# An attention and mixture-of-experts layer: experts' results with slots on partitions, added up in the output's rows by transfers

## The chip, the cores and the metric

The kernel runs on one core of a Trainium2 chip. The metric is the device time of one execution in microseconds. The core has TensorE (PE, matmuls and transposes through it, results in PSUM), VectorE (DVE), ScalarE (ACT), GpSimd (POOL) and SyncE (SP); transfers (DMAs) are issued by SP, ACT and POOL and carried by 16 DMA engines. Each engine works through its own queue in order, and waits on semaphores for the others.

## The reference

The input x has 16 sequences of 256 tokens with 128 channels, 4096 tokens in all. The result is x plus an attention branch and a mixture-of-experts branch, both on the normalised x. Cut to what matters:

```python
xn = layernorm(x)                                  # per token
# attention: 16 heads of 8 channels, causal, relu on q, k, v
att = softmax(mask(q @ k.T / sqrt(8))) @ v + xn
att = gamma * normalise(att) + beta
# experts: RMS norm, 8 experts, the best two per token
h = rms_weight * xn * rsqrt(mean(xn**2) + 1e-6)
w, i = top_2(softmax(h @ gate_w.T)); w = w / w.sum()
for each expert e:
    eo[e] = (silu(h @ w1[e].T) * (h @ w3[e].T)) @ w2[e].T
out = x + att + xn + sum over the token's two experts of w * eo[e]
```

An expert has 448 hidden units. A token's expert output thus counts for the two experts that it was routed to, 8192 results of 128 channels in all.

## The kernel before, in words

**Layout.** Tokens lie on partitions, 32 token tiles of 128, in 8 blocks of four (`BT`). The first part of the kernel normalises x (`normed`, `exact`), routes tokens (`route`), and writes each token's normalised row, its number and its weight into the list of each of its two experts (`scattered`): the dram tensor `lists` has rows of 130 floats, 128 channels, the token's place (`C`) and its weight (`C + 1`), and is filled by indirect transfers from POOL (L612). The place is made by an iota (L604): row p * 32 + t for partition p of token tile t. Places that no token fills hold numbers from 4096 on (`filling`).

**Attention.** The main loop runs over 16 units `u`, two halves of the heads for each of the 8 blocks. A unit has scores and their maxima, `weights` (three parts: ScalarE's exponentials `e`, from unit 3 on with the causal mask by POOL's L884), `values` (L899, L910) that read the masked `e`, and `finish` (L929 transposes, VectorE normalises). TensorE's order is the program's own, written by hand; a scheduler orders the other engines. Between pieces of a unit, `fill` puts other work: normalisation, logits, steps of the experts and one step of `rest`.

**Experts.** `experts` is a generator with three steps for each of 36 tiles of 256 list places (more, if the routing needs them, in a branch at the end). `fetch` loads a tile's rows (`frows`) and the expert's weights by SP, two tiles ahead. `turned_rows` transposes the rows (L1112). `up` multiplies by w1 and w3 (L1123), and ScalarE and VectorE form `hid` (L1131, L1132, L1134), hidden units on partitions. `down` multiplies by w2 (L1140): w2 is the stationary operand, the result has channels on partitions and the 256 places in columns, and ScalarE copies it to SBUF as `yT` (L1148). `deliver`, one step later, transposes `yT` back by two PE transposes (L1154), so that places lie on partitions, VectorE multiplies by each place's weight (`fres`, L1156), and POOL issues two indirect transfers with accumulation (L1160), 128 rows of 512 B each, into rows of the dram tensor `places`. As a token has results in two tiles, a tile's transfers wait until those of the tile before have landed; within a tile they don't wait for each other.

**PSUM.** `misc` has two buffers in turn, for logits, projections, transposes, `values`, and here the down product and the transposed result. `fres` and `yT` have two buffers each.

**Rest of the layer.** `rest(n0, n1)` normalises the attention result of blocks n0 to n1 (small VectorE operations, then ScalarE L1218, L1223 and VectorE L1219, L1224, L1225) and leaves in `y` everything of the output but the experts' part. It runs a step at a time beside the main loop from block 5 on: `rest(0, 4)` from then, `rest(4, 6)` in the last unit, `rest(6, 8)` after it, a step for each remaining step of the experts.

**Beginning and end.** `places` is zeroed by nine SP stores (L269, L272), the ninth for the 256 rows that unfilled places write to. At the end, behind the last scatter, eight transfers by SP and ACT load `places` in the order of `y` (L1370), VectorE adds (L1374), and SP and ACT store to `out` (L1375).

Of the kernel before, what the change touches and what calls it, by code (L numbers as in the profile page):

```python
# [9 lines left out]
F32 = mybir.dt.float32  # L10
# [4 lines left out]
ALU = mybir.AluOpType  # L15
AX = mybir.AxisListType

P = 128
# [8 lines left out]
def tile_attention_plus_moe(  # L27
# [31 lines left out]
    nc = tc.nc  # L59
    V, S, G, T = nc.vector, nc.scalar, nc.gpsimd, nc.tensor  # L60

    NTOK, C = x.shape
    NT = NTOK // P
# [3 lines left out]
    NCI = w2T.shape[2]  # L67
    I = CI * NCI
    BT = 4
    BW = BT * P  # L70
    NB = NT // BT
# [17 lines left out]
    SL = 256  # L89
# [16 lines left out]
    y = const.tile([P, NT, C], F32, name="y")  # L106
# [71 lines left out]
    ident = const.tile([P, P], F32, name="ident")  # L178
# [78 lines left out]
    nought = const.tile([P, BW], F32, name="nought")  # L257
# [6 lines left out]
    G.memset(taken, 0.0)  # L264
    lists = tc.dram_tile([E * CAP + SL, RW], F32, name="lists")

    places = tc.dram_tile([NTOK + SL, C], F32, name="places")
    for a in range(0, NTOK, BW):
        nc.sync.dma_start(  # L269
            out=places[a : a + BW, :].rearrange("(p t) c -> p (t c)", p=P), in_=nought  # L270
        )
    nc.sync.dma_start(  # L272
        out=places[NTOK : NTOK + SL, :].rearrange("(p t) c -> p (t c)", p=P),
        in_=nought[:, 0 : SL // P * C],
    )
    fill_ins = nc.sync.dma_start(
        out=lists[E * CAP : E * CAP + SL, :].rearrange("(a p) w -> p a w", p=P), in_=filling
    )
# [27 lines left out]
    def misc(name):  # L306
        return psM.tile([P, BW], F32, tag="misc", name=name)
# [275 lines left out]
    def scattered(part, t0, at_u, wts):  # L583

        t1 = ROUTES[part][1]
        for b0 in range(t0, t1, 2 * BT):
            blocks = range(b0, min(b0 + 2 * BT, t1), BT)  # L590
            rows = {}
            for r in range(2):
                for b in blocks:
                    if r == 0:
                        rows[b] = norm.tile([P, BT, RW], F32, tag="rows", bufs=4, name=f"rows_{b}")
                        for t in range(BT):
                            S.activation(
                                rows[b][:, t, 0:C],
                                xn[:, b + t, :],
                                AF.Copy,  # L600
                                scale=rstd[:, b + t : b + t + 1],
                            )
                    if r == 0:
                        G.iota(  # L604
                            rows[b][:, :, C].bitcast(I32),
                            [[1, BT]],
                            base=b,
                            channel_multiplier=NT,
                        )
                    G.tensor_copy(rows[b][:, :, C + 1], wts[:, r, b - t0 : b - t0 + BT])  # L610
                    for t in range(BT):
                        ins = G.indirect_dma_start(  # L612
                            out=lists,
                            out_offset=bass.IndirectOffsetOnAxis(
                                ap=at_u[:, r, b - t0 + t : b - t0 + t + 1], axis=0
                            ),
                            in_=rows[b][:, t, :],
                            in_offset=None,
                        ).ins
                        tc.declare_no_dep(  # L620
                            ins, group="lists", reason="lists' rows are written once"
                        )
                        tc.add_to_no_dep_group("lists", ins)
                        tc.add_to_no_dep_group(f"rows of part {part}", ins)
                        yield ins
# [188 lines left out]
    turned = {}  # L814
# [246 lines left out]
    def experts(ffn, i0, i1):  # L1061
# [3 lines left out]
        NH = SL // P  # L1065
# [69 lines left out]
            return h  # L1135

        def down(i, hid, w2, rows):
            yp = misc(f"Y_{i}")[:, :SL]
            for c in range(NCI):
                T.matmul(  # L1140
                    yp,
                    lhsT=w2[:, 0, c, :],
                    rhs=hid[c // 2][:, ts(c % 2, SL)],
                    start=(c == 0),
                    stop=(c == NCI - 1),
                )
            yT = ffn.tile([P, SL], F32, tag="yT", bufs=2, name=f"yT_{i}")
            S.copy(yT, yp)  # L1148
            return yT, rows

        def deliver(i, yT, rows):
            tp = misc(f"R_ps_{i}")[:, :SL].rearrange("p (a c) -> p a c", c=C)
            for a in range(NH):
                T.transpose(tp[:, a, :], yT[:, ts(a, P)], ident)  # L1154
            res = ffn.tile([P, NH, C], F32, tag="fres", bufs=2, name=f"fres_{i}")
            V.tensor_tensor(  # L1156
                res, tp, rows[:, :, C + 1 : C + 2].to_broadcast([P, NH, C]), ALU.mult
            )
            for a in range(NH):
                ins = G.indirect_dma_start(  # L1160
                    out=places,
                    out_offset=bass.IndirectOffsetOnAxis(
                        ap=rows[:, a, C : C + 1].bitcast(U32), axis=0
                    ),
                    in_=res[:, a, :],
                    in_offset=None,
                    compute_op=ALU.add,
                ).ins
                tc.declare_no_dep(
                    ins, group=f"results of tile {i}", reason="a list has a token once"  # L1170
                )
                tc.add_to_no_dep_group(f"results of tile {i}", ins)
            behind["POOL"] = ins
# [1 line left out]
        got = {i: fetch(i) for i in range(i0, min(i0 + 2, i1))}  # L1175
        yield
        hT = turned_rows(i0, got[i0][0])
        late = turned = None
        for i in range(i0, i1):
            if turned is not None:  # L1180
                deliver(*turned)
            rows, w1, w3, w2 = got.pop(i)
            if i + 2 < i1:
                got[i + 2] = fetch(i + 2)
            hid = [up(i, 0, hT, w1, w3)]
            yield
            if late is not None:
                turned = (late[0], *down(*late))
            if i + 1 < i1:
                next_hT = turned_rows(i + 1, got[i + 1][0])  # L1190
            yield
            hid.append(up(i, 1, hT, w1, w3))
            hT = next_hT
            late = (i, hid, w2, rows)
            yield
        if turned is not None:
            deliver(*turned)
        turned = (late[0], *down(*late))
        yield
        deliver(*turned)  # L1200

    rstd2 = const.tile([P, NT], F32, name="rstd2")
    nmean2 = const.tile([P, NT], F32, name="nmean2")
# [1 line left out]
    def rest(n0, n1):  # L1205

        t0, t1 = n0 * BT, n1 * BT
        lv = small.tile([P, t1 - t0], F32, tag="lv", name=f"lv_{n0}")
        V.tensor_scalar(lv, mv[:, t0:t1, 1], LN2_EPS, None, ALU.add)
        _, rl = yield from newton_sqrt(lv[:], t1 - t0, "l")  # L1210
        nm = small.tile([P, t1 - t0], F32, tag="nm", name=f"nm_{n0}")
        V.scalar_tensor_tensor(nm, mv[:, t0:t1, 0], -1.0, rl, ALU.mult, ALU.mult)
        yield
        for n in range(n0, n1):
            yn = y[:, ts(n, BT), :]
            for t in range(n * BT, n * BT + BT):
                i = slice(t - t0, t - t0 + 1)
                S.activation(y[:, t, :], y[:, t, :], AF.Identity, bias=nm[:, i], scale=rl[:, i])  # L1218
            V.tensor_tensor(yn, yn, gamma_sb.unsqueeze(1).to_broadcast([P, BT, C]), ALU.mult)  # L1219
            yield  # L1220
            for t in range(n * BT, n * BT + BT):
                by, mean = agains[t]
                S.activation(xn[:, t, :], xn[:, t, :], AF.Identity, bias=mean, scale=by)  # L1223
            V.tensor_tensor(yn, yn, beta_sb.unsqueeze(1).to_broadcast([P, BT, C]), ALU.add)  # L1224
            V.tensor_tensor(yn, yn, xn[:, ts(n, BT), :], ALU.add)  # L1225
            yield


    def chain(*parts):
# [70 lines left out]
    for u in range(len(units)):  # L1300
        n, r = units[u]
# [41 lines left out]
            side["rest"] = rest(0, 4) if n == 5 else rest(4, 6)  # L1343
    side["rest"] = chain(side["rest"], rest(6, 8))
    for _ in side["experts"]:
        next(side["rest"], None)
    for _ in side["rest"]:
        pass

# [10 lines left out]

    early.__exit__(None, None, None)
    late_pool.__exit__(None, None, None)
    last = ctx.enter_context(tc.tile_pool(name="last", bufs=NB, reuse_waits="tile"))
    ov = out.rearrange("(t p) c -> p t c", p=P)
    pv = places[0:NTOK, :].rearrange("(p t) c -> p t c", p=P)
    zs = []
    for n in range(NB):
        z = last.tile([P, BT, C], F32, tag="z", name=f"z_{n}")
        eng = nc.sync if n % 2 == 0 else nc.scalar
        eng.dma_start(out=z, in_=pv[:, ts(n, BT)])  # L1370
        zs.append(z)
    for n in range(NB):
        yn = y[:, ts(n, BT), :]
        V.tensor_tensor(yn, yn, zs[n], ALU.add)  # L1374
        (nc.sync if n % 2 == 0 else nc.scalar).dma_start(out=ov[:, ts(n, BT), :], in_=yn)  # L1375


# [50 lines left out]
```

## Time and profile before

| what | value |
| --- | --- |
| median of 6 runs | 646.78 us (644.81 to 651.02) |
| the profiled execution's own time | 648.49 us |
| its span | 646.7 us |
| granted TensorE clock, mean | 0.935 of full |
| busy: PE, DVE, ACT, POOL | 542.8, 432.9, 338.3, 265.5 us |
| POOL's accumulating scatters, L1160 | 72 of 1.589 us in the mean, 3.3 us from issue to landing (median) |
| zeroing stores, L269 | 8 of 256 KB, 3.1 us to landing |
| first and last of L1160 issued | 181.7 and 627.3 us |

How to read the lines: times are microseconds from the span's start. A group's line has the source line, engine, operation, tiles (output <- input), shapes and count; then busy time in all and mean nanoseconds of one; then the time that the engine stood idle just before, and what ended most of it. An f32 matmul is recorded as two instructions, a transpose as one. In a timeline's line the brackets hold the idle time before it and what ended it; that releaser is inferred, and of several it is the one seen last. A row by stage has, after its borders and length, the busy time and count of PE, of PE's weight loads, DVE, ACT and POOL, then the granted clock, the share of the DMA engines and GB/s. An "issue" of a POOL transfer is the time in which POOL makes its descriptors; the transfer lands later.

### The profile page before, as it was taken

The page shows a single profiled execution, that of the slowest core. Times are in us where ns is not written, and L with a number is a line of the kernel's source. Part 1 is how long each engine was busy: PE and PEld are TensorE (multiplying, and loading weights), DVE is VectorE, ACT ScalarE, POOL GpSimd, SP SyncE. Part 2 cuts the span into 40 slices and gives each one's busy share as a digit, 9 for nine tenths or more (in the row PEclk, how much of TensorE's full clock was granted, in tenths as well). Part 3 has the DMA queues.
Part 4 walks back from the last instruction along what each step waited for, and adds up shares of the span by engine and source line. Part 5 has one row for each costly group of instructions (what it writes and reads, how often), then busy time and mean ns, then how long its engine had stood idle before and what let it go on. Part 6 is the DMA issues. An engine that isn't in the chain of part 4 may idle for free. (4 is left out here: it accounts for less than half of the span.)

```text
span 646.7 us, 9948 instructions
## 1 busy us (share of the span) xinstructions
PE 542.8 (84%) x3269; PEld 322.7 (50%) x3283; DVE 432.9 (67%) x1153; ACT 338.3 (52%) x677; POOL 265.5 (41%) x311
## 2 busy tenths in 40 slices
PE   3587879669988889899999999899989998999920
PEld 1244434335655545565556555555655565666610
DVE  6758688655577866868576847693787556665833
ACT  1534796456527446564555455536478554446520
POOL 4240027730125866566435332444235342445440
PEclk9796779779989989999999999999999999999975
DMA  6200001143023433353333324232332232435128
GB/s 196 106 1 1 2 16 42 51 137 102 15 45 88 116 84 73 87 127 89 87 85 67 71 60 103 60 67 64 95 73 60 60 67 69 103 63 119 14 25 260
DMA packets 45893, 49.34 MB, mean 76 GB/s; under 512 B 5840, under 2 KB 38224, under 8 KB 45840
## 3 DMA queue, kind: packets, MB, share of 16 engines
q1 hardware_dynamic: 30112, 37.40, 19.4%
q0 software_dynamic: 12416, 8.99, 10.0%
q10 hardware_dynamic: 3312, 2.30, 1.2%
q8 instruction: 27, 0.44, 0.3%
q14 instruction: 26, 0.21, 0.1%
HBM read 34.16 MB, written 14.50 MB: 75 GB/s over the span
## 5 line engine op out<-in xcount | busy, mean ns | idle before, releaser
L1160 POOL DMA_INDIRECT places<-fres,frows x72 | 114.4, 1589 | 115.3 <-DVE fres L1156 82.4
L1123 PE MATMUL AG<-hT,w 128*112 128x256 f32 x576 | 143.5, 394 | 8.2 <-PE R_ps L1154 5.4
L884 POOL TENSOR_SCALAR_AFFINE_SELECT e<-e 128x512 f32<-128x512 f32 (+1 forms) x78 | 70.2, 950 | 153.4 <-ACT e L881 152.8
L1123 PEld LDWEIGHTS AG<-hT,w 128*112 128x112 f32 x576 | 100.3, 182 | 43.6 <-issue 10.9
L881 ACT ACTIVATE e<-W 128x1024 f32<-128x1024 f32 x96 | 93.4, 1020 | 38.9 <-PE W L855 25.8
L1132 DVE SCALAR_TENSOR_TENSOR th<-th,AG 112x512 f32<-112x512 f32 x72 | 49.4, 686 | 74.5 <-ACT th L1131 73.6
L805 DVE TENSOR_REDUCE tops<-S 128x4 f32<-128x1024 f32 x64 | 75.3, 1217 | 32.8 <-PE S L783 32.8
L1131 ACT ACTIVATE th<-AG 112x512 f32<-112x512 f32 x72 | 42.7, 593 | 66.2 <-PE AG L1123 65.7
L1140 PE MATMUL Y<-hid,w 112*128 112x256 f32 x288 | 70.2, 386 | 6.4 <-DVE Qs L823 3.1
L612 POOL DMA_INDIRECT lists<-rows,ratu_c x64 | 64.8, 1012 | 21.9 <-issue 14.7
L770 PE MATMUL S<-KTm,QT 32*128 32x256 f32 (+1 forms) x512 | 70.6, 545 | 3.5 <-DVE tops L805 2.3
L855 PE MATMUL W<-Qm,KT 32*128 32x512 f32 (+1 forms) x512 | 61.7, 536 | 3.0 <-DVE tops L805 2.3
L1140 PEld LDWEIGHTS Y<-hid,w 112*128 112x128 f32 x288 | 52.1, 190 | 21.7 <-PE q_ps L700 4.3
L1134 DVE TENSOR_TENSOR hid<-th,AG 112x512 f32<-112x512 f32 x72 | 48.9, 679 | 1.6
L770 PEld LDWEIGHTS S<-KTm,QT 32*128 32x128 f32 x512 | 31.4, 194 | 24.1 <-issue 12.1
L920 ACT COPY oT<-O 128x512 f32<-128x512 f32 x32 | 18.7, 584 | 46.3 <-PE O L910 46.3
L899 PE MATMUL O<-e,vstat 128*32 128x512 f32 x256 | 36.1, 634 | 8.1 <-DVE rs L940 4.7
L797 DVE TENSOR_REDUCE tops<-S 128x8 f32<-128x1024 f32 x32 | 37.6, 1216 | 2.1 <-PE S L783 2.1
L783 PE MATMUL S<-cmask,ident_bf 128*128 128x256 bf16 (+1 forms) x192 | 37.4, 319 | 0.0
L1148 ACT COPY yT<-Y 128x256 f32<-128x256 f32 x36 | 13.3, 369 | 40.9 <-PE Y L1140 40.7
L855 PEld LDWEIGHTS W<-Qm,KT 32*128 32x128 f32 x512 | 24.7, 190 | 18.0 <-issue 5.5
L783 PEld LDWEIGHTS <-ident_bf 128*128 128x128 bf16 x192 | 15.1, 99 | 35.9 <-issue 31.5
(241 smaller groups left out, 758.0 us busy)
## 6 DMA issues: line engine op xcount, KB each, us to landing
w<-in_w1T_dram SPq DMA_DIRECT2D x36, 224.0 KB, 2.6
w<-in_w3T_dram SPq DMA_DIRECT2D x36, 224.0 KB, 3.2
w<-in_w2T_dram SPq DMA_DIRECT2D x36, 224.0 KB, 3.4
frows<-lists SPq DMA_DIRECT2D x36, 130.0 KB, 2.1
places<-nought SPq DMA_DIRECT2D x8, 256.0 KB, 3.1
lists<-filling SPq DMA_DIRECT2D x9, 130.0 KB, 2.9
places<-fres,frows POOLq DMA_INDIRECT x72, 3.3
lists<-rows,ratu_c POOLq DMA_INDIRECT x64, 2.4
```

The source lines that it names most:

```text
L612: ins = G.indirect_dma_start(out=lists, out_offset=bass.IndirectOffsetOnAxis(ap=at_u[:, r, b - t0 + t : b - t0 + t + 1], axis=0), in_=rows ...
L770: T.matmul(out, lhsT=QT[rows, q0 : q0 + P], rhs=KTm[rows, :, b * SEQ : b * SEQ + nk], start=(part < 2 or b == 0), stop=False, skip_group_c ...
L783: T.matmul(out, lhsT=ident_bf, rhs=cmask[:, 0, :].unsqueeze(1).to_broadcast([P, 4 if part == 2 else 2, P]), start=False, stop=True, skip_g ...
L805: ins = V.tensor_reduce(of_heads[:, :, part, 1, :], pairs[g // 2].rearrange("p g (j k) -> p g j k", j=HG), AX.X, ALU.max, negate=True,).ins
L855: T.matmul(out, lhsT=KT[rows, k0 : k0 + P], rhs=Qm[rows, :, k0 : (b + 1) * SEQ], start=(part > 0 or b == 0), stop=on_pool and (part > 0 or ...
L881: ins = S.activation(two, pairs[g // 2], AF.Exp).ins
L884: behind["POOL"] = G.affine_select(on, on, [[0, 2 * nd], [1, P]], ALU.is_ge, no_weight, base=0, channel_multiplier=-1).ins
L1123: T.matmul(to[:, ts(c, SL)], lhsT=wt[:, 0, ts(2 * k + c, CI)], rhs=hT, start=True, stop=True,)
L1132: V.scalar_tensor_tensor(th, th, 1.0, ap, ALU.add, ALU.mult)
L1134: V.tensor_tensor(h, th, gp, ALU.mult)
L1140: T.matmul(yp, lhsT=w2[:, 0, c, :], rhs=hid[c // 2][:, ts(c % 2, SL)], start=(c == 0), stop=(c == NCI - 1),)
L1160: ins = G.indirect_dma_start(out=places, out_offset=bass.IndirectOffsetOnAxis(ap=rows[:, a, C : C + 1].bitcast(U32), axis=0), in_=res[:, a ...
```

## The change

The experts' results are made with list places on partitions at once. In `down`, `hid` becomes the stationary operand (128 places at a time) and w2 the moving one; for each half `a` of the places, four products add up over the hidden units. The two transposes, the copy `yT` and the step between `down` and `deliver` are gone; VectorE's product with the weights reads the down product from PSUM, and the scatters follow.

The scatters accumulate into `out` itself, whose rows are zeroed at the start in place of `places`. The iota therefore makes the token's own row number, t * 128 + p. Unfilled places have numbers over the last row, and a bounds check leaves them out, so the ninth zeroing store is gone.

`rest` adds each finished block of `y` to `out` by a transfer with accumulation from POOL, 256 KB each. The loads, sums and stores at the end are gone. After the main loop, `rest` goes two steps for each step of the experts.

All transfers to `out` are kept in order where they overlap: in the order that is built, an accumulating transfer of `rest` stands in POOL's queue behind a wait for the scatters before it, and the scatter after it waits for it. Two transfers of `rest` with no scatter between them don't wait for each other. Of the eight, those of blocks 0 to 3 stand in the main loop (units 12 and 13), those of 4 and 5 after tile 32's scatters, those of 6 and 7 after tile 33's and tile 34's.

```diff
-    places = tc.dram_tile([NTOK + SL, C], F32, name="places")
+    ov = out.rearrange("(t p) c -> p t c", p=P)
     for a in range(0, NTOK, BW):
         nc.sync.dma_start(
-            out=places[a : a + BW, :].rearrange("(p t) c -> p (t c)", p=P), in_=nought
+            out=out[a : a + BW, :].rearrange("(p t) c -> p (t c)", p=P), in_=nought
         )
-    nc.sync.dma_start(
-        out=places[NTOK : NTOK + SL, :].rearrange("(p t) c -> p (t c)", p=P),
-        in_=nought[:, 0 : SL // P * C],
-    )
...
                         G.iota(
                             rows[b][:, :, C].bitcast(I32),
-                            [[1, BT]],
-                            base=b,
-                            channel_multiplier=NT,
+                            [[P, BT]],
+                            base=b * P,
+                            channel_multiplier=1,
                         )
...
         def down(i, hid, w2, rows):
-            yp = misc(f"Y_{i}")[:, :SL]
-            for c in range(NCI):
-                T.matmul(
-                    yp,
-                    lhsT=w2[:, 0, c, :],
-                    rhs=hid[c // 2][:, ts(c % 2, SL)],
-                    start=(c == 0),
-                    stop=(c == NCI - 1),
-                )
-            yT = ffn.tile([P, SL], F32, tag="yT", bufs=2, name=f"yT_{i}")
-            S.copy(yT, yp)
-            return yT, rows
-
-        def deliver(i, yT, rows):
-            tp = misc(f"R_ps_{i}")[:, :SL].rearrange("p (a c) -> p a c", c=C)
+
+            yp = misc(f"Y_{i}")[:, :SL].rearrange("p (a c) -> p a c", c=C)
             for a in range(NH):
-                T.transpose(tp[:, a, :], yT[:, ts(a, P)], ident)
+                for c in range(NCI):
+                    k = c % 2 * SL + a * P
+                    T.matmul(
+                        yp[:, a, :],
+                        lhsT=hid[c // 2][:, k : k + P],
+                        rhs=w2[:, 0, c, :],
+                        start=(c == 0),
+                        stop=(c == NCI - 1),
+                    )
             res = ffn.tile([P, NH, C], F32, tag="fres", bufs=2, name=f"fres_{i}")
             V.tensor_tensor(
-                res, tp, rows[:, :, C + 1 : C + 2].to_broadcast([P, NH, C]), ALU.mult
+                res, yp, rows[:, :, C + 1 : C + 2].to_broadcast([P, NH, C]), ALU.mult
             )
             for a in range(NH):
                 ins = G.indirect_dma_start(
-                    out=places,
+                    out=out,
...
                     in_offset=None,
+                    bounds_check=NTOK - 1,
+                    oob_is_err=False,
                     compute_op=ALU.add,
                 ).ins
...
-        late = turned = None
+        late = None
         for i in range(i0, i1):
-            if turned is not None:
-                deliver(*turned)
...
             if late is not None:
-                turned = (late[0], *down(*late))
+                down(*late)
...
-        if turned is not None:
-            deliver(*turned)
-        turned = (late[0], *down(*late))
-        yield
-        deliver(*turned)
+        down(*late)
...
             V.tensor_tensor(yn, yn, xn[:, ts(n, BT), :], ALU.add)
             yield
+            G.dma_start(out=ov[:, ts(n, BT), :], in_=yn, accum_op=ALU.add)
...
     for _ in side["experts"]:
-        next(side["rest"], None)
+        for _ in range(2):
+            next(side["rest"], None)
...
-    last = ctx.enter_context(tc.tile_pool(name="last", bufs=NB, reuse_waits="tile"))
-    ov = out.rearrange("(t p) c -> p t c", p=P)
-    pv = places[0:NTOK, :].rearrange("(p t) c -> p t c", p=P)
-    zs = []
-    for n in range(NB):
-        z = last.tile([P, BT, C], F32, tag="z", name=f"z_{n}")
-        eng = nc.sync if n % 2 == 0 else nc.scalar
-        eng.dma_start(out=z, in_=pv[:, ts(n, BT)])
-        zs.append(z)
-    for n in range(NB):
-        yn = y[:, ts(n, BT), :]
-        V.tensor_tensor(yn, yn, zs[n], ALU.add)
-        (nc.sync if n % 2 == 0 else nc.scalar).dma_start(out=ov[:, ts(n, BT), :], in_=yn)
```

## The prediction

> **What bounds the kernel now.** I read the chain that ended last first, then GpSimd's (POOL's) timeline at the end, then the busy time by stage, then the costliest groups kept apart by shape. Tiles of 256 list places are numbered 0 to 35.
>
> The chain that ended last, in order of time (start, length, what):
>
> ```profile
> 606.50 24.16 DMA places<-fres,frows x2
> ...
> 631.79 5.95 DMA z<-places
> 637.74 0.02 issue
> 637.76 1.14 DVE y L1374 x2
> ```
>
> From 606.50 to 630.65 the chain is nothing but scatters: a tile's scatter waits until the one before has landed. Then the sums are loaded back, added, and stored. POOL's timeline at the end:
>
> ```profile
> 606.50 1.55 POOL L1160 DMA_INDIRECT places<-fres,frows  x1 [6.56 <-DVE rs L940]
> 608.36 1.55 POOL L1160 DMA_INDIRECT places<-fres,frows  x1 [0.30 <-issue]
> 612.36 1.55 POOL L1160 DMA_INDIRECT places<-fres,frows  x1 [2.45 <-DVE l_s L295]
> 614.22 1.55 POOL L1160 DMA_INDIRECT places<-fres,frows  x1 [0.30 <-issue]
> 618.14 1.55 POOL L1160 DMA_INDIRECT places<-fres,frows  x1 [2.37 <-DVE th L1132]
> ...
> 627.34 1.55 POOL L1160 DMA_INDIRECT places<-fres,frows  x1 [0.31 <-issue]
> ```
>
> These are tiles 32, 33, 34 and the last of 35. The step from tile 33 to 34 is 5.78 us: 1.86 between the two scatters, 3.3 from the second's issue to its landing, 0.7 until the next is issued. Before that, TensorE sets the pace (stage, length, PE busy):
>
> ```profile
> 300.00:460.00 160.00, 150.52 (x941) 92.12 (x947) 107.77 (x252) 87.98 (x159) 62.85 (x56) 1.00 0.32 74
> 460.00:600.00 140.00, 132.43 (x840) 82.32 (x840) 92.14 (x191) 80.63 (x147) 59.30 (x50) 1.00 0.35 77
> ```
>
> PE is busy 94% of both stages. The rows that the sums below use:
>
> ```profile
> L1140 PE MATMUL Y<-hid,w 112*128 112x256 f32 x288 | 70.2, 386 | 6.4 <-DVE Qs L823 3.1 <-DVE hid L1134 2.2 <-DVE fres L1156 0.2
> L1154 PE MATMUL R_ps<-ident,yT 128*128 128x128 f32 x72 | 14.6, 284 | 4.7 <-DVE Qs L823 2.2 <-DVE lraw L662 1.7 <-ACT yT L1148 0.5
> L737 PE MATMUL v_ps<-wv_in,xnT 128*128 128x128 f32 x64 | 10.4, 284 | 0.0
> L1148 ACT COPY yT<-Y 128x256 f32<-128x256 f32 x36 | 13.3, 369 | 40.9 <-PE Y L1140 40.7
> L612 POOL DMA_INDIRECT lists<-rows,ratu_c x64 | 64.8, 1012 | 21.9 <-issue 14.7 <-DVE step L1001 4.2 <-DMA lists<-rows,ratu_c 1.2
> ```
>
> **TensorE and ScalarE.** Each tile loses two transposes (L1154) and one copy (L1148). In the trace, from a tile's first transpose to the start of the next matmul is at least 0.22 us in all 36 tiles, 17.9 us over all; what exceeds 0.22 is the next matmul waiting, and that wait may stay. About 33 tiles lie before the chained end: 33 x 0.22 = -7.3 us (at most -16.4). The down product goes from 8 recorded passes of 256 columns, starting 0.216 apart (1.73 us), to 16 passes of 128. The nearest row, L737, has the same f32 product with 128 moving columns and a new weight each time; its passes start 0.112 us apart, so 16 x 0.112 = 1.79 us. That is +0.06 x 33 = +2.0 us. Its weight loads last 192 ns each (112x128 in L1140: 190); if they did not overlap, a tile would take 16 x 0.19 = 3.0 us. The copies are off the path (ScalarE is busy 52%): 0. But Y's PSUM buffer is now freed by VectorE's product (fres) instead of the copy, and the `misc` pool has two. L899 waits 3.4 us in all for the copy; the product, behind VectorE's queue, may wait longer: I take +0.5 us, bounds -3.4 and +12 (0.35 x 36).
>
> **Scatters.** Still 72, with the same payload. The product follows the down matmuls at once, so a tile's scatter starts some 5 us earlier. I leave the bounds check at nothing (bounds -0.54 and +0.54 each, the difference of L1160 and L612; eight of them at the end give 4 us). VectorE's product waits for the scatter two tiles back to release `fres`; at the end that is tile 33 for tile 35, and only the last tile's own work is behind it.
>
> **Zeroing and the final sums.** One of nine zeroing stores goes; these end before 25 us and the first scatter is at 181.7, so that cover makes it 0. At the end, four groups go: eight loads of z, eight VectorE sums, eight stores, and their waits. The last scatter lands at 630.65 and the last store's packets end at 644.7. The program ends at 646.7.
>
> **The eight accumulating transfers.** They are issued by POOL, each of 256 KB as 512 rows of 512 B. In the built order each waits for the last scatter to land, and the next scatter waits for it. The trace has no direct transfer from POOL. Its issue D lies between 1.0 us (L612, a plain scatter of 128 rows) and 6.2 us (four times the 1.55 of L1160, since it has four times the rows). I take 1.55: the same engine and the same accumulation. After the issue the trace gives 0.55 us to the first packet and 0.45 from the last packet to landing; 8 packets per DMA engine take 0.79 us, 65 ns each once they run, so 32 take 2.4 to 3.2, I take 2.5. One transfer therefore lands D + 3.5 = 5.05 us after its start, and 0.7 later the next scatter starts.
>
> A rule from the Trainium skill (DMA: Bandwidth & Descriptors, Anatomy of one DMA) sets a POOL transfer at 2.0 us plus bytes/436e3. For the scatter's 64 KB it gives 2.15 us, and the trace shows 3.3. For 256 KB it gives 2.6 us, an estimate that would take some 8 us off the end; I don't use it.
>
> In the main loop four of these stand in front of the masks of e (L884). Laid on the trace of before: transfer 0 waits for a scatter until 483.7 and holds POOL to 485.3; e_0's masks, ready at 484.0, are needed at 501.0: no loss. Transfer 1 goes in between e_1's two masks; the second ends by 499.2 instead of 494.1, needed at 501.0. Transfer 2 and the next scatter pair push e_2's masks to 509 to 511, needed at 511.1. At unit 14 a scatter pair now stands before e_2's masks and delays them by some 1.9 us. I take +1 us for the loop; with D at 6.2, +8, because e_2's masks then end near 519.
>
> So the loop gives s = -7.3 + 2.0 + 0.5 + 1.0 = about **-4 us** (bounds -10 and +13).
>
> **The end.** After the last masks (598 to 600) stand five tiles' results less one: tiles 32 to 35, with transfers 4 and 5 between 32 and 33, transfer 6 before 34, transfer 7 before 35. In before's time: Y of tile 32 ends 598.65, VectorE is free at 600.1, scatter at 600.8. Plus 5.86 (1.86 + 3.3 + 0.7): transfer 4 at 606.7, transfer 5 at 608.5; its packets go behind the first one's and land at 614.2. Tile 33 at 614.9, transfer 6 at 620.8 (block 6's sum ended at 619.4 in before, and the rest now goes two steps at a time), tile 34 at 626.5, transfer 7 at 632.4, tile 35 at 638.1, landing +1.86 + 3.3 = 643.3. In before POOL's drain ended 1.7 us after the last scatter's landing, and 1.3 us of barrier close the span: +3.0, 646.3. Less 4: **642.3**, against a span of 646.7. That execution took 648.49 us and the median of runs is 646.78, about its span. So I put -4.4 on the median: **642.4 us**. What the loads and stores gave back at the end (14 us) is thus taken up by four transfers in the scatters' chain; the net comes from TensorE.
>
> **Rivals.** *The issue of the accumulations decides, and it is slower.* The place is POOL's queue in the last 40 us. Each us of D costs about 3.6 us there and 1.2 us in the loop; slower than before from D of 2.5 us. For it: accumulating 128 rows costs 0.54 us more than L612's plain ones, and 1.0 + 4 x 0.54 gives 3.2. Against: a semaphore increment on POOL with no rows lasts 1.01 us in the trace, just what L612 takes, so rows may cost little. At 3.9 (halfway between 1.55 and 6.2): 642.3 + 4.8 x 2.35 = 653.6; at 6.2, 668.
>
> *A wash.* D near 2.2 (+3.1), or TensorE's gain lost to VectorE's late release of Y: 646. For it: the end alone sums to 646.3, nothing gained. Against: PE is busy 94% where the transposes go.
>
> *Weight loads are not hidden in the shorter down product.* 33 x (3.0 - 1.73 - 0.22) = +35 us, some 680. Against: L737's 0.112 us.
>
> *It frees more.* All waits behind the transposes go too (-9 us more) and D is 1.0: 632.
>
> **How the numbers follow.** About 3.2 us, 0.5%, is what a measurement can tell. Forecast (638 to 643.5): 0.38. Wash: 0.20. Slow issue: 0.33. Loads: 0.03. Frees more: 0.06. Faster by over 0.5%: 0.38 + 0.06 = 0.44; within: 0.20; slower: 0.36. The range goes from 636 to 658: below is most of the last case, above are D over 4.9 and the weight loads, together under 0.2. The likeliest case's own range is 638 to 643.5.
>
> **What would show it.** POOL's row for the direct transfers: mean near 1.55 us, landing near 5. Down passes 0.112 us apart. In the chain at the end: scatters of tiles 33, 34 and 35 about 12 us apart, with a transfer in between. The last masks end some 4 us earlier than 600. If the direct issue is over 2.5 us, or POOL's masks show waits by PE of more than 5 us in all, the forecast is wrong.

## The result, and the profile after

The changed kernel takes 651.57 us (median of 20 runs, 650.06 to 655.89) against 646.89 us for the kernel before (46 runs, 644.64 to 651.75): a ratio of 1.0062, 95% interval 1.0045 to 1.0080. It is 0.6% slower, where 0.7% faster was forecast; the time lies inside the range given. Its profiled span is 649.2 us, against 646.7 before and a predicted 642.3. Here and below, ratios leave out executions over 1.5% above the fastest of the same kernel and so aren't exactly the quotients of the medians; the trace of e10 below is of such an execution.

The end is where the change was expected to give and take most. POOL's timeline of the changed kernel from the last masks on (start, length, instruction, in brackets the idle time before):

```profile
603.34 0.63 POOL L880 TENSOR_SCALAR_AFFINE_SELECT e<-e 128x512 f32<-128x512 f32 x1 [3.28 <-ACT e L877]
604.24 0.63 POOL L880 TENSOR_SCALAR_AFFINE_SELECT e<-e 128x512 f32<-128x512 f32 x1 [0.28 <-ACT e L877]
606.58 1.64 POOL L1151 DMA_INDIRECT out_dram<-fres,frows  x1 [1.70 <-DVE mv L962]
608.52 1.96 POOL L1151 DMA_INDIRECT out_dram<-fres,frows  x1 [0.30 <-issue]
612.66 2.69 POOL L1214 DMA_DIRECT2D out_dram<-y  x2 [2.19 <-DVE y L950]
620.02 1.65 POOL L1151 DMA_INDIRECT out_dram<-fres,frows  x1 [4.67 <-DVE nm L1199]
...
630.57 1.64 POOL L1151 DMA_INDIRECT out_dram<-fres,frows  x1 [3.21 <-DMA out_dram<-y]
...
641.66 1.65 POOL L1151 DMA_INDIRECT out_dram<-fres,frows  x1 [3.94 <-DMA out_dram<-y]
```

The chain is the predicted one: scatters of tiles 32 to 35 with transfers in between, 13.4, 10.6 and 11.1 us from tile to tile. From tile 32's scatter to the end of the span it takes 649.2 - 606.58 = 42.6 us, where 646.3 - 600.8 = 45.5 was worked out. The direct transfers are even cheaper than taken. From the page's groups and from its list of transfers (last number: us to landing):

```profile
L1151 POOL DMA_INDIRECT out_dram<-fres,frows x72 | 115.1, 1599 | 122.4 <-DVE fres L1147 67.6
...
L1139 PE MATMUL Y<-w,hid 112*128 112x128 f32 x576 | 73.7, 282 | 8.5 <-DVE hid L1130 4.7
...
out_dram<-y POOLq DMA_DIRECT2D x8, 256.0 KB, 4.5
```

So the end isn't what went wrong. Tile 32's scatter was expected at 600.8 - 4 = 596.8 and came at 606.58, 9.8 us late. The delay was made earlier: the last exponentials start at 602.24 (596.43 before), 5.8 us later where 4 us earlier were forecast, again 9.8. Even that flatters the forecast: the changed kernel begins unit 3 2.3 us earlier (first exponentials at 162.52, before 164.83), which the forecast didn't have. From there to the last exponentials it takes 439.7 us against 431.6, 8.1 more where 4 less were forecast. The waits by the engine that waits and what it waited for (us in all, times, longest) have rows that the kernel before doesn't have; this is the largest. Changed kernel:

```profile
PE hT_ps L1108 <- DVE vb L737: 8.7, 4, 3.0
```

Kernel before, the same transposes:

```profile
PE hT_ps L1112 <- ACT yT L1148: 1.8, 4, 0.5
```

The timeline shows one of the four. Changed kernel:

```profile
261.52 1.95 PE L1139 MATMUL Y<-w,hid 112*128 112x128 f32 x16
...
262.90 0.69 DVE L1130 TENSOR_TENSOR hid<-th,AG 112x512 f32<-112x512 f32 x1
263.51 2.35 DVE L801 TENSOR_REDUCE tops<-S 128x4 f32<-128x1024 f32 x2
...
266.01 0.42 DVE L737 TENSOR_TENSOR vb<-v_ps,bv_sb 128x256 f32<-128x256 f32 x1
...
266.49 0.69 PE L1108 MATMUL hT_ps<-ident,frows 128*128 128x128 f32 x2 [3.02 <-DVE vb L737]
266.50 0.42 DVE L1147 TENSOR_TENSOR fres<-Y,frows 128x256 f32<-128x256 f32 x1
```

The kernel before, at the same point of its program:

```profile
263.12 0.37 ACT L1148 COPY yT<-Y 128x256 f32<-128x256 f32 x1 [1.27 <-PE Y L1140]
263.20 2.35 DVE L805 TENSOR_REDUCE tops<-S 128x4 f32<-128x1024 f32 x2
...
263.54 0.44 PE L1112 MATMUL hT_ps<-ident,frows 128*128 128x128 f32 x2 [0.46 <-ACT yT L1148]
...
265.70 0.42 DVE L741 TENSOR_TENSOR vb<-v_ps,bv_sb 128x256 f32<-128x256 f32 x1
```

TensorE writes v_ps, then Y, then hT_ps, and `misc` has two buffers. Before, VectorE emptied one (vb) and ScalarE the other (yT). While VectorE was in its two reductions (2.35 us), ScalarE's copy let the transposes through at 263.54. After, VectorE empties both, vb and fres, behind the same reductions, and TensorE stands still from 263.5 to 266.5. What lets the transposes through then is vb, which ends at 266.43; fres only starts at 266.50. So what was lost is the early emptying by ScalarE, and TensorE is thrown back on one that came late in both kernels.

Another of the four is as long:

```profile
180.19 1.95 PE L1139 MATMUL Y<-w,hid 112*128 112x128 f32 x16
...
180.84 2.35 DVE L801 TENSOR_REDUCE tops<-S 128x4 f32<-128x1024 f32 x2
...
184.65 0.42 DVE L737 TENSOR_TENSOR vb<-v_ps,bv_sb 128x256 f32<-128x256 f32 x1
...
185.12 0.69 PE L1108 MATMUL hT_ps<-ident,frows 128*128 128x128 f32 x2 [2.98 <-DVE vb L737]
```

Here the reductions end at 183.2, and vb stands behind another 1.5 us of small VectorE instructions.

What follows is the clock. The changed kernel by stage around these two gaps of 3.0 us (3.3 from the start of Y's last pass; borders, length, busy time and count of PE, weight loads, DVE, ACT, POOL; then the granted clock):

```profile
177.40:184.20 6.80, 4.74 (x37) 3.33 (x35) 5.80 (x17) 1.11 (x3) 0.31 (x1) 1.00 0.01 4
184.20:191.00 6.80, 5.88 (x30) 2.40 (x34) 3.35 (x9) 0.89 (x2) 3.34 (x3) 0.50 0.22 20
...
259.30:266.10 6.80, 4.17 (x34) 2.93 (x32) 4.89 (x14) 1.77 (x5) 3.06 (x4) 1.00 0.09 29
266.10:272.90 6.80, 6.41 (x34) 2.61 (x38) 3.73 (x11) 0.89 (x2) 3.19 (x2) 0.50 0.66 109
```

TensorE ran at half clock for 6.8 us behind each gap. Between unit 3's first exponentials and unit 15's last, the kernel before has 6.8 us at half clock, the changed one 20.5.

### The profile page after: what moved, and what is told of

It reads as the page before. It is cut to its first block, busy times and chain, and to the rows that moved or that the text cites. A ratio compares the mean times of both kernels' runs of the same rounds, so it can differ in the third digit from the quotient of the medians.

```text
span 649.2 us, 10354 instructions
## 1 busy us (share of the span) xinstructions
PE 542.3 (84%) x3485; PEld 330.0 (51%) x3499; DVE 424.9 (65%) x1145; ACT 327.9 (51%) x641; POOL 274.4 (42%) x319
## 4 chain that ended last, share of the span: by engine, by line
PE 54%; DVE 24%; ACT 8%; DMA 6%; issue 4%; POOL 3%; SPq 0%; ACTq 0%; DVEq 0%; POOLq 0%
PE AG L1119 17%; PE S L766 7%; PE Y L1139 6%; PE W L851 5%; PE O L895 4%; PE S L779 4%; DMA out_dram<-fres,frows 4%; DVE tops L801 3%; PE q_ps L696 3%; DVE th L1128 3%; DVE hid L1130 2%; DVE tops L793 2%; PE O L906 2%; POOL lists L608 2%; PE k_ps L709 2%
## 5 line engine op out<-in xcount | busy, mean ns | idle before, releaser
L1151 POOL DMA_INDIRECT out_dram<-fres,frows x72 | 115.1, 1599 | 122.4 <-DVE fres L1147 67.6
L1119 PEld LDWEIGHTS AG<-hT,w 128*112 128x112 f32 x576 | 100.7, 182 | 54.2 <-issue 20.5
L801 DVE TENSOR_REDUCE tops<-S 128x4 f32<-128x1024 f32 x64 | 75.3, 1216 | 17.1 <-PE S L779 17.1
L1139 PE MATMUL Y<-w,hid 112*128 112x128 f32 x576 | 73.7, 282 | 8.5 <-DVE hid L1130 4.7
L1139 PEld LDWEIGHTS Y<-w,hid 112*128 112x128 f32 x576 | 69.0, 195 | 18.0 <-DVE hid L1130 5.1
L895 PE MATMUL O<-e,vstat 128*32 128x512 f32 x256 | 38.1, 660 | 9.2 <-DVE rs L936 4.7
L779 PE MATMUL S<-cmask,ident_bf 128*128 128x256 bf16 (+1 forms) x192 | 39.1, 329 | 0.0
L1110 ACT ACTIVATE hT<-hT_ps,rw_sb 128x256 f32<-128x256 f32 x36 | 17.0, 471 | 37.5 <-PE hT_ps L1108 37.4
```

The lines of the kernel that those rows point to most:

```text
L779: T.matmul(out, lhsT=ident_bf, rhs=cmask[:, 0, :].unsqueeze(1).to_broadcast([P, 4 if part == 2 else 2, P]), start=False, stop=True, skip_g ...
L801: ins = V.tensor_reduce(of_heads[:, :, part, 1, :], pairs[g // 2].rearrange("p g (j k) -> p g j k", j=HG), AX.X, ALU.max, negate=True,).ins
L895: T.matmul(op[rows, :], lhsT=v[:, 2 * b, r * NG + g, :], rhs=e0[:, g, :], start=True, stop=False, skip_group_check=True, tile_position=(0, ...
L1119: T.matmul(to[:, ts(c, SL)], lhsT=wt[:, 0, ts(2 * k + c, CI)], rhs=hT, start=True, stop=True,)
L1139: T.matmul(yp[:, a, :], lhsT=hid[c // 2][:, k : k + P], rhs=w2[:, 0, c, :], start=(c == 0), stop=(c == NCI - 1),)
L1151: ins = G.indirect_dma_start(out=out, out_offset=bass.IndirectOffsetOnAxis(ap=rows[:, a, C : C + 1].bitcast(U32), axis=0), in_=res[:, a, : ...
```

## The experiments

The runs were made in groups, each with its own runs of the kernel before, whose median was 646.9 to 660.9 us from group to group. So ratios are taken within a group: e1 to e4 are one, e5, e6, e7 and e9 another, e8, e10 and e11 a third. In the profiles, much of that spread lies ahead of unit 3, whose first exponentials start at 162.5 to 176.3 us. The loop is therefore compared from there to the last part of unit 15, which I call the loop below, and the end from tile 32's scatter to the end of the span. My theory from the two traces: TensorE waits because VectorE now empties both `misc` buffers. The rivals: POOL's earlier scatters and the added transfers, or the product's new shape in itself.

### One half of the change at a time

**Form alone** (e1): the kernel before with the new product; `places`, the final loads and sums stay.

```diff
-            yp = misc(f"Y_{i}")[:, :SL]
-            for c in range(NCI):
...
-            S.copy(yT, yp)
...
+            yp = misc(f"Y_{i}")[:, :SL].rearrange("p (a c) -> p a c", c=C)
             for a in range(NH):
-                T.transpose(tp[:, a, :], yT[:, ts(a, P)], ident)
+                for c in range(NCI):
+                    k = c % 2 * SL + a * P
+                    T.matmul(
+                        yp[:, a, :],
+                        lhsT=hid[c // 2][:, k : k + P],
+                        rhs=w2[:, 0, c, :],
...
```

> Only the new down product and the earlier scatter; results still go to places and are loaded and added at the end, as in the kernel before. Buffer theory (without the transposes, the product Y and the transposed rows hT follow v_ps in the two misc buffers, so that hT waits for VectorE to empty v_ps, four times, 9 us in all, and the two longest waits bring half-clock stretches): those waits are here too, the last masks end near 604 as in the changed kernel, the time is 645 to 648. POOL theory (the accumulating transfers from POOL hold up the masks of e in the loop): the loop is not longer than before, the last masks end at 595 to 599, the time is 637 to 643.

**Sums alone** (e2): the product and the transposes of before; scatters go into `out`, eight accumulating transfers replace the loads and sums.

```diff
-                    out=places,
+                    out=out,
...
+            G.dma_start(out=ov[:, ts(n, BT), :], in_=yn, accum_op=ALU.add)
```

> Only the accumulation into out and the transfers of the rest; the down product, copy and transposes as in the kernel before. Buffer theory: no wait of hT for v_ps of the changed kernel's kind, the last masks end near 600 as before, and the end's chain alone gives 646 to 650. POOL theory: the last masks end at 604 or later and the time is 651 or more.

Measured beside the kernel before at 660.93 us: e1 665.33 us, ratio 1.0061 (1.0021 to 1.0100); e2 662.10 us, ratio 1.0010 (0.9979 to 1.0040). e1 waits exactly as the changed kernel does:

```profile
PE hT_ps L1112 <- DVE vb L741: 8.7, 4, 3.0
```

e2 keeps the old row, 1.9 us for ScalarE's copy. e1's loop takes 445.1 us with 23.9 at half clock, e2's 436.8 with 6.8. So the loss sits in the form, and the sums by transfers come out about even, as their end alone was predicted to (646.3 of 646.7). The times expected for e1, 645 to 648, are 0.997 to 1.002 of the kernel before's 646.9: e1 came out slower than the buffer theory had it, e2 within it.

### Fewer transfers

e4 is the changed kernel with block 0's transfer only.

```diff
-            G.dma_start(out=ov[:, ts(n, BT), :], in_=yn, accum_op=ALU.add)
+            if n == 0:
+                G.dma_start(out=ov[:, ts(n, BT), :], in_=yn, accum_op=ALU.add)
```

> The changed kernel with only block 0's accumulating transfer; blocks 1 to 7 of the output lack everything but the experts' part. Buffer theory: the loop's loss stays, last masks near 604, and only the end's chain shortens, by some 20 us: a span near 632. POOL theory: the loop's loss goes too, last masks at 598 or before, a span near 625.

One execution took 645.49 us. The end takes 31.4 us (612.42 to 643.8), 11.2 less than the changed kernel's 42.6 (some 20 less were expected): that is about the price of the four transfers there. The wait of hT_ps for vb stays at 8.7 us in 4, so POOL's transfers don't make it. The loop takes 437.3 us against 439.7, with 10.2 us at half clock instead of 20.5. So the same waits can bring more or less time at half clock.

### Taking the wait away, first attempt

e3 puts Y and the next tile's hT_ps in the two halves of one `misc` buffer, so that the transposes need no second one.

```diff
+            both = misc(f"YH_{i}")
             if late is not None:
-                down(*late)
+                down(*late, both)
             if i + 1 < i1:
-                next_hT = turned_rows(i + 1, got[i + 1][0])
+                next_hT = turned_rows(i + 1, got[i + 1][0], both)
```

> The changed kernel, but Y and the transposed rows hT of the next tile lie in the two halves of one misc buffer, so that hT no longer needs the buffer of v_ps. Buffer theory: the waits of hT for v_ps (9 us) and the half-clock stretches behind them go, the last masks end at 594 to 598, the time is 638 to 644, under the kernel before. POOL theory: the masks are as late as in the changed kernel, 649 to 653.

687.59 us, ratio 1.0412 (1.0355 to 1.0469): a miss. The wait for vb is gone, but another came in its place:

```profile
PE YH L1108 <- DVE fres L1147: 36.9, 34, 3.7
```

As built, TensorE's write into one half waits for VectorE's read of the other half, which stands before it in the program, and so in nearly every tile instead of in four. The remedy failed; the price of letting TensorE wait for VectorE's emptying shows all the more: the loop takes 467.8 us.

The Trainium skill (Perfetto Trace Analysis, Optimizing Tensor Performance) says that independent groups of matmuls should go round through different PSUM banks, so that emptying one overlaps the next. e3, with two groups in one buffer, waits 36.9 us, in agreement, though e6 below, with the same buffer and another order, doesn't wait. But the changed kernel does go round through two buffers, and waits all the same, 8.7 us, where one engine empties both.

### Taking the wait away, second attempt, in two ways

e5 gives the product with the weights to ScalarE, the engine that emptied Y before:

```diff
-            V.tensor_tensor(
-                res, yp, rows[:, :, C + 1 : C + 2].to_broadcast([P, NH, C]), ALU.mult
-            )
+            for a in range(NH):
+                S.activation(
+                    res[:, a, :], yp[:, a, :], AF.Copy, scale=rows[:, a, C + 1 : C + 2]
+                )
```

> The changed kernel, but the product with the places' weights is made by ScalarE (two activations of 128x128 with a scale per partition, in place of one VectorE product), so that Y's PSUM buffer is emptied by the engine that emptied it before the change. Theory (TensorE waits for VectorE, which now empties both misc buffers in a row; some 9 us of waits, and half-clock stretches behind the two long ones): the waits of hT_ps for vb shrink from 8.7 us to under 2.5 us, the gaps of 3.3 us behind Y in units 3 to 5 are gone, the loop is 6 to 10 us shorter than that of the changed kernel, ratio to the kernel before 0.988 to 0.997. Rival (the product with 128 moving columns, or scatter pairs that stand earlier in POOL's queue, in front of the masks, slow the loop by themselves): the loop stays as long, ratio 1.003 to 1.009. Second rival (72 more ScalarE instructions of about 0.3 us delay the exponentials, ScalarE having lost only 36 of 0.37 us): 1.00 to 1.01 with the waits for vb gone and longer waits on ScalarE's e.

e6 is e3 with the product and the scatters (`deliver`) moved behind the transposes:

```diff
-                down(*late, both)
+            made = down(*late, both) if late is not None else None
             if i + 1 < i1:
                 next_hT = turned_rows(i + 1, got[i + 1][0], both)
+            if made is not None:
+                deliver(*made)
```

> The changed kernel with Y of one tile and the next tile's hT_ps in two halves of one misc buffer, and VectorE's product placed behind the transposes in the program, so that the transposes wait neither for vb nor for the product. Theory (VectorE's late emptying of two buffers in a row costs TensorE the time): no hT_ps wait for vb, none for fres; the loop is 6 to 10 us shorter than that of the changed kernel, ratio to the kernel before 0.988 to 0.997. What could spoil it: the next tile's products or the next v_ps now wait for the buffer instead; then that wait shows by name and the ratio is 1.00 or more. Rival (the shape of the product or POOL's order): waits gone, loop as long as the changed kernel's, 1.003 to 1.009.

Beside them ran the changed kernel once more:

> The changed kernel as it is, on the chip of the runs beside it, so that they can be compared with it directly. Expected: ratio to the kernel before 1.004 to 1.009, hT_ps waits for vb of 8 to 10 us, half-clock stretches behind the 3.3 us gaps. If the half-clock stretches are missing while the waits are there, the stretches belong to the first execution alone and the waits must explain the loss.

| kernel (before: 650.03 us) | median us | ratio, interval | loop us | of it at half clock | waits of hT_ps for emptying |
| --- | --- | --- | --- | --- | --- |
| changed again (e9) | 652.74 | 1.0034, 1.0003 to 1.0066 | 440.3 | 20.5 | 8.7 |
| product by ScalarE (e5) | 646.64 | 0.9933, 0.9904 to 0.9963 | 432.9 | 10.2 | 4.4 |
| one buffer, product later (e6) | 643.26 | 0.9880, 0.9846 to 0.9915 | 427.3 | 6.8 | 0 |

(The kernel before's first profile has 431.6 and 6.8; its waits are 1.8.) e5's four and a half:

```profile
PE hT_ps L1108 <- ACT fres L1148: 3.3, 3, 1.9
PE hT_ps L1108 <- DVE vb L737: 1.1, 1, 1.1
```

e9's stage that holds the two gaps, with the granted clock behind POOL's numbers:

```profile
170.00:300.00 130.00, 112.80 (x718) 69.45 (x720) 91.11 (x276) 62.44 (x121) 70.96 (x75) 0.92 0.38 87
```

The same stage of e6:

```profile
170.00:300.00 130.00, 117.25 (x817) 75.23 (x821) 99.16 (x286) 64.96 (x127) 76.39 (x79) 0.99 0.39 90
```

The product's shape, the scatters and all eight transfers are the changed kernel's in both, and both are faster than it: by 7.4 and 12.9 us of loop, where 6 to 10 were expected. With the shape or POOL's order as the cause, the loops would have stayed. e5 gets about half of e6's gain: it has ScalarE's waits instead, and TensorE's L895 waits 5.4 us for ScalarE's fres (2.2 for VectorE's in e9).

### Putting the wait into the kernel before

The reverse test changes one word in the kernel before: VectorE copies Y instead of ScalarE.

```diff
-            S.copy(yT, yp)
+            V.tensor_copy(yT, yp)
```

> The kernel before the change with one word changed: Y is copied out of PSUM by VectorE instead of ScalarE. Product, transposes, scatters and the end are those of before. Theory (what cost the loop is that Y's buffer is emptied by VectorE, late): the waits of TensorE's hT_ps for VectorE (vb or the copy) come up here too, 6 to 10 us in all, with gaps of about 3.3 us in the units 2 to 5 and half-clock stretches behind them, and the loop is 6 to 11 us longer, ratio 1.009 to 1.018. Rival (the wait is only there with the new product or the earlier scatters): ratio 0.998 to 1.004 and no such waits.

675.16 us against 660.28, ratio 1.0194 (1.0138 to 1.0250): slower than the range that was expected, though the interval reaches into it. The transposes wait for VectorE in 4 places, 8.7 us in all, as in the changed kernel:

```profile
PE hT_ps L1112 <- DVE vb L741: 5.6, 3, 2.5
...
PE hT_ps L1112 <- DVE lh_s L330: 3.1, 1, 3.1
```

Its loop takes 450.0 us, 17.1 at half clock. The nearest to set that against is e2, which has the old product and ScalarE's copy and whose kernel before took as long: 436.8. Nothing of the change is in e10, so who empties Y is enough to bring the wait and a loss. The edit also moves 36 copies into VectorE's queue (305.9 us busy in the loop, 293.9 in the kernel before); what part of the loss these make by other ways than this wait isn't separated.

### A shorter end

Three kernels rearrange the transfers. e7 is e5, e8 is e6, each with the rest of blocks 4 and 5 begun one unit half earlier (their transfers go out in the loop) and blocks 6 and 7 issued back to back. e11 is e6 with blocks 4 to 7 issued in a row in front of tile 35. The edit of e7 and e8:

```diff
-            G.dma_start(out=ov[:, ts(n, BT), :], in_=yn, accum_op=ALU.add)
+            if n0 < 6:
+                G.dma_start(out=ov[:, ts(n, BT), :], in_=yn, accum_op=ALU.add)
+        for n in range(max(n0, 6), n1):
+            G.dma_start(out=ov[:, ts(n, BT), :], in_=y[:, ts(n, BT), :], accum_op=ALU.add)
...
-        if r == 0 and n in (5, 7):
+        if (n, r) in ((5, 0), (6, 1)):
```

and of e11:

```diff
-            G.dma_start(out=ov[:, ts(n, BT), :], in_=yn, accum_op=ALU.add)
+            if n0 < 4:
+                G.dma_start(out=ov[:, ts(n, BT), :], in_=yn, accum_op=ALU.add)
+        if n0 == 6:
+            for n in range(4, 8):
+                G.dma_start(out=ov[:, ts(n, BT), :], in_=y[:, ts(n, BT), :], accum_op=ALU.add)
```

> The kernel of e5_scalar, and the transfers of blocks 4 and 5 start in the loop (their part of the rest one unit half earlier) and those of blocks 6 and 7 are issued back to back, so that of the scatters' chain at the end only one transfer's length is left beside the last four tiles. If the end is the chain that was predicted (42.6 us from tile 32's scatter to the end of the span, about 5.7 us for each place at which transfers stand between two tiles), it is 10 to 13 us shorter than e5_scalar's: 30 to 33 us. With the theory of the loop, ratio to the kernel before 0.970 to 0.982; if the loop's loss isn't the buffer's, 0.983 to 0.993; if VectorE's earlier work of the rest takes the place of the gain, 0.99 or more.

> e6_one_buffer_late with the end of e7_scalar_early: transfers of blocks 4 and 5 in the loop, in front of the last unit's last masks, those of 6 and 7 back to back before tile 35. From the two measured parts (0.988 and the 6.4 us between the spans of e5 and e7): ratio 0.975 to 0.982; the last masks come some 4 to 5 us later than in e6, as in e7. If the early transfers delay the masks more here, where the loop is shorter and has less slack, 0.983 to 0.988.

> e6_one_buffer_late with the transfers of blocks 4 to 7 all issued together, behind tile 34's scatters and in front of tile 35's: nothing is put in front of the last masks, and the chain is broken at one place instead of three. Three places cost 17.3 us in e5 (7.0, 5.0 and 5.2 from a transfer's start to the next scatter's); four transfers in a row take 4 x 1.35 us of issue and some 4.5 to 8 us to the last landing, 10 to 13 us in all. Expected: the last masks as in e6, the span 4 to 7 us shorter than e6's, ratio 0.977 to 0.983. Rival (four transfers share the DMA engines, 2.5 us of packets each, and the last one lands over 10 us after its issue): no gain, 0.985 to 0.99.

| kernel | median us | before, same group | ratio, interval | end us |
| --- | --- | --- | --- | --- |
| e5 | 646.64 | 650.03 | 0.9933, 0.9904 to 0.9963 | 42.9 |
| e7 | 640.03 | 650.03 | 0.9850, 0.9812 to 0.9887 | 35.3 |
| e6 | 643.26 | 650.03 | 0.9880, 0.9846 to 0.9915 | 44.0 |
| e8 | 647.89 | 660.28 | 0.9814, 0.9776 to 0.9852 | 35.9 |
| e11 | 650.17 | 660.28 | 0.9853, 0.9808 to 0.9897 | 37.2 |

e7's end is 7.6 us shorter than e5's, not the 10 to 13 that I expected. In its POOL timeline tile 33 waits for its product, so the scatters' chain no longer sets that step:

```profile
603.61 1.57 POOL L1152 DMA_INDIRECT out_dram<-fres,frows  x1 [1.33 <-ACT fres L1148]
...
611.82 1.55 POOL L1152 DMA_INDIRECT out_dram<-fres,frows  x1 [4.79 <-ACT fres L1148]
```

Its two early transfers also stand in front of the last unit's masks and delay the last exponentials (the loop takes 436.2 us, e5's 432.9, and 6.8 us at half clock lie there, from 587.6). So its ratio, 0.9850, misses the expected 0.970 to 0.982 and falls where the case was put in which the loop's loss isn't the buffer's. It doesn't speak for that case: e7's transposes wait as e5's do, 4.4 us. e11's four in a row hold the chain from 632.07 to 642.52, 10.4 us, within what was expected. Its end is 6.8 us shorter than e6's, but its ratio misses the expected 0.977 to 0.983, which its interval reaches. Its loop took 431.6 us in that group, e6's 427.3 in the other, though nothing in it differs up to the last unit; so a few us of loop can't be told from such differences. e8 met its range. All five beat the kernel before and, by their ratios, the changed one (1.0062, again 1.0034); between e7, e8, e11 and e6 the intervals overlap.

## Why the prediction was wrong

**The step that failed** is the term for Y's buffer in the sum for the loop: "But Y's PSUM buffer is now freed by VectorE's product (fres) instead of the copy, and the `misc` pool has two", taken as "+0.5 us, bounds -3.4 and +12". From e6, which has the change without the wait, to the changed kernel beside it, the loop grows by 12.9 us; by the medians it is 652.74 - 643.26 = 9.5. With e5, which keeps half of the waits, it is 7.4 and 6.1. So the term is about +10, near the end of its bounds that I didn't take, and its form was wrong too. I had spread a delay of 0.35 us over 36 tiles, and looked only at L899, the reader of the copy's row in the waits. The wait came in four places, 1.4 to 3.3 us each from the start of Y's last pass to the transposes, and at another instruction, hT_ps, which needs a `misc` buffer right behind Y. The profile of before had what it takes: the second timeline above shows hT_ps let through at 263.54 by ScalarE, and VectorE not free to empty a buffer before 265.70.

**The transposes and the product** (-7.3 + 2.0) and the masks (+1.0) make -4.3 without the failed term. e6's loop is 4.3 us shorter than the one in the first profile of before (427.3 and 431.6). That fits, though the loop of e11, the same program up to the last unit, took 431.6 in another group, so the fit is good to some 4 us and in part luck. Y's 16 passes take 1.95 us in the changed kernel's timeline, not the 3.0 of exposed weight loads: that rival is out.

**The masks of e.** TensorE's waits for POOL's masked e are 4.6 us (matmuls and weight loads, 1.0 before), under the 5 that I had named as the sign of an error; the last unit's first exponentials come 1.7 us later, set against the unit ahead of it, than in the kernel before (33.1 us behind unit 14's, 31.4 before). +1 was predicted. e1, without a transfer into `out` in POOL's queue, has the same 33.1, e2, with all of them, 31.4. So the 1.7 us come with the new product and its earlier scatters, not with the transfers. TensorE's longest wait for a mask in that stretch is 0.9 us for the matmuls; that the rest is the masks' isn't shown.

**The end.** Predicted 45.5 us, measured 42.6, which hid 2.9 us of the miss in the loop. The direct issue has a median of 1.365 us for the 1.55 taken, and the landing comes 4.5 us after the start, for 5.05. The rival with a slow issue (from 2.5 us) gave the right sign for a wrong reason: POOL's queue was quicker than forecast. (Two slips of the sums bear on nothing here: by the prices given, D at 6.2 makes 665 to 666, not 668, and 0.35 x 36 is 12.6, not 12.)

**The wash** named the right mechanism, TensorE's gain lost to VectorE's late release, but capped it at the gain. It cost twice that.

**How the loss divides.** The loops of e9 (first) and e6 (second), whole, in the columns of the stages above:

```profile
163.03:603.29 440.26, 401.69 (x2711) 252.34 (x2723) 291.96 (x717) 225.89 (x404) 201.22 (x187) 0.98 0.35 79
167.57:594.89 427.32, 396.66 (x2712) 251.37 (x2723) 293.36 (x717) 225.79 (x404) 201.89 (x187) 0.99 0.37 81
```

TensorE has the same instructions in both. Of the 12.9 us between them it is busy for 5.0 more, which goes with 13.7 us more at half clock, and stands still for the other 7.9. So standing still is the larger part.

**What stays open** is how much of the clock's part a wait of this size brings. e1 and e4, in one group, have the same four waits of 8.7 us, but 23.9 and 10.2 us at half clock, and their loops are 7.8 us apart, 5.9 of them in TensorE's busy time (404.1 and 398.2). POOL's work in the loop differs little between them: e1 has no transfer of `y`, e4 one. A kernel with the gaps and no half clock, or the reverse, wasn't made.

## What to carry to other kernels

When a change moves the reading of a PSUM buffer from one engine to another, don't price the instruction: list who takes that buffer next, and look in the timeline at what the new reader's queue holds just then. In this kernel a pool with two buffers was only as good as two engines emptying them; with one engine, what stood in that engine's queue became TensorE's wait. And take the waits from the places where they would arise: an average over tiles hides four gaps of up to 3 us.

## What the runs showed of the hardware that wasn't expected

Two gaps were followed by 6.8 us at half clock each in the changed kernel. The last matmul before the first gap ended at 182.14 (180.19 + 1.95) and the clock fell at 184.17, so an idle time of 2.0 us was enough there. The Trainium skill (TensorE: Matmul & The Clock Gate, What's actually happening) has the clock fall after an idle window of about 3.4 us, which runs freely and isn't started by the kernel. The lengths fit that: 3.41 or 6.83 us in every stretch at half clock within the loop. So do the times: the four falls in the changed kernel's loop, at 184.17, 197.83, 235.37 and 266.09 us, lie 4, 11 and 9 times 3.41 us apart. The fall after 2.0 us shows that a whole window's length of idleness isn't needed. In the 3.41 us ahead of these four falls TensorE was busy for 1.33, 1.53, 1.41 and 0.74 us; the emptiest such stretch of the loop at full clock without a fall behind it, from 334.41, had 1.86. That isn't a limit for all runs: e6's clock fell at 487.27 behind 2.09 us of work. How long a stretch follows isn't fixed by the gap: in e4 the same two waits were followed by 3.41 us each.

An accumulating transfer of 256 KB from POOL took less time to issue (median 1.37 us) than a scatter of 64 KB (mean 1.60), although it has four times the rows.
